# Layer norms on GpSimd: negating the mean in an operation of its own and adding it, instead of subtracting it

## The chip, the cores and the metric

The kernel runs on one core of a Trainium2 chip. The metric is the device time of one execution in microseconds (us); lower is better. The fast runs of one kernel in one group of rounds lie within 0.4% of each other here (4233.40 to 4249.76 us is the widest spread). Ratios are the mean time of one kernel's fast runs over the mean of the other kernel's fast runs of the same rounds, so they are not quite the ratio of the medians that are quoted beside them. A run's state was "fast" everywhere below except where it says otherwise; one run of the kernel before, in the rounds of e5 to e8, was slow (6478.50 us at a clock of 0.827) and counts in no ratio.

The engines are named as in the profile: PE is TensorE (matmuls), PEld its weight loads, DVE VectorE, ACT ScalarE, POOL GpSimd, SP the engine that issues transfers. "L314" is line 314 of the kernel's source. The changed kernel has one more line, so its lines from 311 on are shifted by one.

## The reference

Three transformer layers with a masked attention over a graph, then one graph-attention layer, over a batch of 16 sequences of 1024 nodes with 128 features. What matters here is the norm, which each of the three layers does twice and the last layer once (cut):

```python
def _layer_norm(x, g, b):
    mu = jnp.mean(x, axis=-1, keepdims=True)
    var = jnp.var(x, axis=-1, keepdims=True)
    return (x - mu) * jax.lax.rsqrt(var + LN_EPS) * g + b
# per layer (cut):
scores = jnp.where(mask, -jnp.inf, scores); attn = jax.nn.softmax(scores, axis=-1)
x = _layer_norm(h + (attn_out @ Wo + bo), ln1_g, ln1_b)
x = _layer_norm(x + relu(x @ W1 + b1) @ W2 + b2, ln2_g, ln2_b)
```

All gains are 1 and all shifts 0 in the test's inputs, but the kernel computes them.

## The kernel before

The work is cut into 48 blocks (16 sequences, three layers). A block has 32 steps of attention; each step computes scores for four heads on TensorE, masks and exponentiates them, and multiplies the result with the values on TensorE. Between the steps, the rest of another block (projections, norms, feed-forward, the last layer) is threaded in piece by piece. The norms work on half a sequence at a time: four tiles of 128 rows and 128 features, called a half-norm here. There are 224 of them.

The statistics are VectorE's, the rest of the norm GpSimd's:

```python
def stats(n, ts):
    z, st, mv = n
    for t in range(ts.start, ts.stop):
        nc.vector.bn_stats(st[:, t, :], z[:, t, :])
    for t in range(ts.start, ts.stop):
        nc.vector.bn_aggr(mv[:, t, :], st[:, t, :])       # mean, variance

def normalise(n, ts):                                     # L307 to L314
    z, _, mv = n
    v = mv[:, ts, 1]
    nc.gpsimd.tensor_scalar(v, v, EPS, None, op0=OP.add)
    nc.gpsimd.tensor_tensor(v, v, half_neg[:, ts], OP.pow)
    for t in range(ts.start, ts.stop):
        nc.gpsimd.tensor_scalar(z[:, t, :], z[:, t, :], mv[:, t, 0:1], mv[:, t, 1:2],
                                op0=OP.subtract, op1=OP.mult)
```

GpSimd also masks part of each step's exponentials, and TensorE's next product waits for that:

```python
if on_pool:                                               # in score_step; cut
    nc.scalar.activation(ev, psv, AF.Exp, scale=HD ** -0.5)     # L401
    nc.gpsimd.tensor_mul(ev, ev, m)                             # L402
else:
    nc.vector.tensor_add(ev, psv, m)                            # L404
# later, in av_step:
nc.tensor.matmul(acc[...], v_bufs[m % 2][...], e[:, j, :], start=first, stop=last)   # L421
```

## Time and profile before

| | before |
|---|---|
| time, median of 4 runs | 4239.91 us (4233.33 to 4242.12) |
| span in the profile | 4234.7 us |
| PE busy | 3816.1 us, 90% |
| GpSimd busy | 3698.5 us, 87% |
| of it the norm tiles (L314) | 700.8 us, 896 of 795 ns |
| mean granted TensorE clock | 0.983 of full speed |

"Busy" adds up the durations of an engine's instructions. The share alone doesn't say which engine sets the time; for that one reads the chain of work that ended last, and then single stretches of the timeline. The lines themselves stand in the prediction below.

### The profile page before, as it was taken

To read this page: it belongs to the slowest core of one execution; us is meant where nothing else is said; L and a number is where in the kernel's file an instruction comes from. 1 tells how busy PE (TensorE), PEld (TensorE's weight loads), DVE (VectorE), ACT (ScalarE), POOL (GpSimd) and SP (SyncE) were. 2 spreads that over 40 slices of the span, in tenths; PEclk is the share of its full clock that TensorE was granted. 3 is DMA by queue.
4 is the path that set the end of the run, shared out by engine and by line. 5 is a ranking of instruction groups with operands and counts; after the bars stand their busy time and mean duration, and the time that the engine had idled before them with its cause. 6 is when DMAs were issued, how large, how long until landed. Compare 5 with 4: busy or idle time off the path is not lost.

```text
span 4234.7 us, 107443 instructions
## 1 busy us (share of the span) xinstructions
PE 3816.1 (90%) x44501; PEld 1544.2 (36%) x44501; DVE 3405.5 (80%) x5324; ACT 3412.0 (81%) x3961; POOL 3698.5 (87%) x2786
## 2 busy tenths in 40 slices
PE   7999999999998999999999889989999989989986
PEld 2333333344443333334444333333434433333435
DVE  6888888878887888887787888888878787888873
ACT  6988888977778988887777888988777688888760
POOL 4899999988889999997888899998888899999885
PEclk9999999999999999999999999999999999999997
DMA  5221222222211221221222221221222112221200
GB/s 148 66 61 45 57 61 53 49 52 56 64 48 48 61 61 46 56 61 47 56 52 51 61 58 44 61 61 42 52 65 58 47 46 56 61 53 49 52 17 18
DMA packets 126287, 233.09 MB, mean 55 GB/s; under 512 B 36704, under 2 KB 75616, under 8 KB 125792
## 3 DMA queue, kind: packets, MB, share of 16 engines
q1 hardware_dynamic: 122896, 225.14, 21.2%
q8 instruction: 352, 5.77, 0.6%
q10 hardware_dynamic: 2896, 1.01, 0.1%
q14 instruction: 143, 1.17, 0.1%
HBM read 15.54 MB, written 8.39 MB: 6 GB/s over the span
## 4 chain that ended last, share of the span: by engine, by line
POOL 43%; PE 38%; DVE 10%; ACT 4%; issue 4%; DMA 1%; SPq 1%; ACTq 0%; DVEq 0%; POOLq 0%
POOL e L402 20%; PE t L271 15%; PE acc L421 12%; POOL x L314 12%; PE s L394 9%; DVE e L404 5%; POOL mv L312 4%; POOL x L318 2%; ACT e L401 2%; POOL x L319 2%; PE t L260 2%; ACT e L416 1%; DVE st L296 1%; POOL A L435 1%; POOL mv L311 1%
## 5 line engine op out<-in xcount | busy, mean ns | idle before, releaser
L404 DVE TENSOR_TENSOR e<-s,mask_add 128x1024 f32<-128x1024 f32 x2112 | 2501.9, 1211 | 510.0 <-PE s L394 430.0
L416 ACT ACTIVATE e<-e 128x1024 f32<-128x1024 f32 x2112 | 2200.6, 1060 | 387.2 <-DVE e L404 368.9
L402 POOL TENSOR_TENSOR e<-e,mask 128x1024 f32<-128x1024 f32 x960 | 2046.0, 2148 | 300.0 <-ACT e L401 297.2
L421 PE MATMUL acc<-e,v 128*17 128x512 f32 x12288 | 1633.9, 604 | 195.9 <-POOL e L402 152.5
L394 PE MATMUL s<-Wq,Wk 64*128 64x512 f32 x6144 | 1193.5, 457 | 72.3 <-ACT e L401 27.9
L401 ACT ACTIVATE e<-s 128x1024 f32<-128x1024 f32 x960 | 980.7, 1022 | 202.5 <-PE s L394 199.9
L394 PEld LDWEIGHTS s<-Wq,Wk 64*128 64x128 f32 x6144 | 492.8, 186 | 1042.8 <-issue 486.1
L314 POOL TENSOR_SCALAR x<-x,mv 128x128 f32<-128x128 f32 x896 | 700.8, 795 | 22.9
L421 PEld LDWEIGHTS acc<-e,v 128*17 128x17 f32 x12288 | 208.1, 95 | 731.8 <-issue 384.7
L271 PE MATMUL t<-hd,e 128*32 128x129 f32 x8192 | 244.8, 276 | 7.1 <-DVE x L596 3.2
L312 POOL TENSOR_TENSOR mv<-mv,half_neg 128x4 f32<-128x4 f32 x224 | 231.9, 1035 | 18.5
L318 POOL TENSOR_TENSOR x<-x,ln_g 128x1024 f32<-128x1024 f32 x97 | 229.4, 2365 | 12.7 <-PE t L260 12.6
L271 PEld LDWEIGHTS t<-hd,e 128*32 128x32 f32 x8192 | 226.7, 111 | 26.8 <-issue 5.3
L303 DVE TENSOR_TENSOR x<-t,x 128x512 f32<-128x512 f32 x192 | 131.7, 686 | 91.0 <-PE t L271 90.1
L271 PE MATMUL t<-x1T,W 128*32 128x512 f32 x1536 | 202.4, 599 | 2.3 <-DVE hd L546 1.0
L296 DVE BATCH_NORM_STATS2 st<-x 128x6 f32<-128x128 f32 x896 | 196.7, 279 | 3.0
L271 PEld LDWEIGHTS t<-W,hT 128*32 128x32 f32 x6144 | 172.7, 111 | 63.5 <-issue 26.5
L260 PE MATMUL t<-identf,x 128*128 128x128 f32 x896 | 155.0, 298 | 39.6 <-DVE x L303 12.6
L271 PE MATMUL t<-W,hT 128*32 128x128 f32 x6144 | 187.1, 274 | 2.7 <-DVE x L303 1.9
L260 PEld LDWEIGHTS t<-identf,x 128*128 128x128 f32 x896 | 99.1, 146 | 236.5 <-issue 78.4
L311 POOL TENSOR_SCALAR mv<-mv 128x4 f32<-128x4 f32 x224 | 52.6, 235 | 151.7 <-DVE mv L298 137.8
L581 DVE SCALAR_TENSOR_TENSOR e<-s,mask 128x1024 f32<-128x1024 f32 x128 | 150.5, 1210 | 5.9 <-PE s L578 5.0
(82 smaller groups left out, 2438.1 us busy)
## 6 DMA issues: line engine op xcount, KB each, us to landing
Wk<-hi SPq DMA_DIRECT2D x384, 128.0 KB
Wk<-lo SPq DMA_DIRECT2D x384, 128.0 KB
Wq<-hi SPq DMA_DIRECT2D x384, 128.0 KB
Wq<-lo SPq DMA_DIRECT2D x384, 128.0 KB
x<-in_x_dram SPq DMA_DIRECT2D x16, 512.0 KB
out_dram<-x SPq DMA_DIRECT2D x31, 256.0 KB
ai<-in_adj_dram SPq DMA_DIRECT2D x8, 512.0 KB
g_rows<-parts SPq DMA_DIRECT2D x124, 4.0 KB
```

What stands on the lines that cost most here:

```text
L260: nc.tensor.transpose(ps[:, t * P:(t + 1) * P], src[:, 4 * h + t, :], identf)
L271: nc.tensor.matmul(dst[j:j + SLOT, :], lhsT[:, j:j + SLOT], rhs, start=start, stop=stop)
L296: nc.vector.bn_stats(st[:, t, :], z[:, t, :])
L312: nc.gpsimd.tensor_tensor(v, v, half_neg[:, ts], OP.pow)
L314: nc.gpsimd.tensor_scalar(z[:, t, :], z[:, t, :], mv[:, t, 0:1], mv[:, t, 1:2], op0=OP.subtract, op1=OP.mult)
L318: nc.gpsimd.tensor_mul(z, z, rows(gain, n))
L394: nc.tensor.matmul(ps[:, r * 512:(r + 1) * 512], k[64 * r:64 * r + 64, kt * P:(kt + 1) * P], q[64 * r:64 * r + 64, q0:q0 + 512], start=Tru ...
L401: nc.scalar.activation(ev, psv, AF.Exp, scale=HD ** -0.5)
L402: nc.gpsimd.tensor_mul(ev, ev, m)
L404: nc.vector.tensor_add(ev, psv, m)
L416: nc.scalar.activation(ev, ev, AF.Exp, scale=HD ** -0.5)
L421: nc.tensor.matmul(acc[j * SLOT:j * SLOT + HD + 1, :], v_bufs[m % 2][:, kt, 2 * j + g, :], e[:, j, :], start=first, stop=last)
```

## The change

The idea: if GpSimd's subtraction with a following multiplication runs in a slow form, write the subtraction as the addition of a negated number, and pay for the negation with one small operation per half-norm.

```diff
-        v = mv[:, ts, 1]
+        m, v = mv[:, ts, 0], mv[:, ts, 1]
+        nc.gpsimd.tensor_scalar(m, m, -1.0, None, op0=OP.mult)
         nc.gpsimd.tensor_scalar(v, v, EPS, None, op0=OP.add)
         nc.gpsimd.tensor_tensor(v, v, half_neg[:, ts], OP.pow)
         for t in range(ts.start, ts.stop):
-            nc.gpsimd.tensor_scalar(z[:, t, :], ..., op0=OP.subtract, op1=OP.mult)
+            nc.gpsimd.tensor_scalar(z[:, t, :], ..., op0=OP.add, op1=OP.mult)
```

The order of all other instructions on each engine is the same in both programs.

More of the change, by code (lines that the diff above doesn't have):

```diff
@@ L313, in normalise @@
         for t in range(ts.start, ts.stop):
-            nc.gpsimd.tensor_scalar(z[:, t, :], z[:, t, :], mv[:, t, 0:1], mv[:, t, 1:2], op0=OP.subtract, op1=OP.mult)
+            nc.gpsimd.tensor_scalar(z[:, t, :], z[:, t, :], mv[:, t, 0:1], mv[:, t, 1:2], op0=OP.add, op1=OP.mult)
     def scale_shift(z, gain, bias):
```

## The prediction

> **What bounds the kernel now.** I read the first page from its top. Busy shares and the 40 slices first, to see whether one engine is the bound:
>
> ```profile
> PE 3816.1 (90%) x44501; PEld 1544.2 (36%) x44501; DVE 3405.5 (80%) x5324; ACT 3412.0 (81%) x3961; POOL 3698.5 (87%) x2786
> ...
> PE   7999999999998999999999889989999989989986
> ...
> POOL 4899999988889999997888899998888899999885
> ```
>
> No engine is alone at the top. TensorE (PE) is busy 90% of a span of 4234.7 us and GpSimd (POOL) 87%, and both stay at 8 to 9 tenths in nearly every slice: there is no stage with a limit of its own, the whole run is one steady interleaving. Next the chain that ended last, to see how those two share the path:
>
> ```profile
> POOL 43%; PE 38%; DVE 10%; ACT 4%; issue 4%; DMA 1%; SPq 1%; ACTq 0%; DVEq 0%; POOLq 0%
> POOL e L402 20%; PE t L271 15%; PE acc L421 12%; POOL x L314 12%; PE s L394 9%; DVE e L404 5%; POOL mv L312 4%; POOL x L318 2%; ACT e L401 2%; POOL x L319 2%; PE t L260 2%; ACT e L416 1%; DVE st L296 1%; POOL A L435 1%; POOL mv L311 1%
> ```
>
> The path changes hands: GpSimd 43%, TensorE 38%. Line 314, the one that the change edits, has 12% of it, some 508 us. The groups of GpSimd's instructions by line give its busy time as 700.8 us, so about 508/700.8 = 0.72 of its time lies on the path. For line 312 the same quotient is 0.04 x 4234.7 / 231.9 = 0.73.
>
> The groups by line, kept apart by shape, give the price of each operation that the change touches or that I compare with:
>
> ```profile
> L402 POOL TENSOR_TENSOR e<-e,mask 128x1024 f32<-128x1024 f32 x960 | 2046.0, 2148 | 300.0 <-ACT e L401 297.2 <-DMA Wq<-lo 1.9
> L314 POOL TENSOR_SCALAR x<-x,mv 128x128 f32<-128x128 f32 x896 | 700.8, 795 | 22.9
> L312 POOL TENSOR_TENSOR mv<-mv,half_neg 128x4 f32<-128x4 f32 x224 | 231.9, 1035 | 18.5
> L311 POOL TENSOR_SCALAR mv<-mv 128x4 f32<-128x4 f32 x224 | 52.6, 235 | 151.7 <-DVE mv L298 137.8 <-DVE chk L326 13.9
> L200 POOL TENSOR_TENSOR b<-b,row 128x128 f32<-128x128 f32 x3 | 1.4, 458 | 15.6 <-DMA row<-in_L_gnn_ln_b_dram 15.6
> ```
>
> Line 314 is 896 one-tensor operations of 128 elements at 795 ns. Line 200, an operation with two tensors on the same 128x128 shape, takes 458 ns. So line 314, with one tensor to read and not two, takes 1.7 times as long. That oddity is what the whole prediction hangs on.
>
> Last the timeline of GpSimd over one group of four tiles and the stretches of 10 us around such bursts:
>
> ```profile
> 2004.82 0.25 POOL L311 TENSOR_SCALAR mv<-mv 128x4 f32<-128x4 f32 x1
> 2005.15 1.04 POOL L312 TENSOR_TENSOR mv<-mv,half_neg 128x4 f32<-128x4 f32 x1
> 2006.29 3.13 POOL L314 TENSOR_SCALAR x<-x,mv 128x128 f32<-128x128 f32 x4
> 2009.39 0.23 POOL L311 TENSOR_SCALAR mv<-mv 128x4 f32<-128x4 f32 x1
> ```
>
> ```profile
> 2060.00:2070.00 10.00, 6.31 (x60) 2.77 (x56) 8.44 (x25) 4.92 (x5) 9.63 (x13) 0.83 0.01 2
> 2070.00:2080.00 10.00, 10.00 (x80) 3.15 (x72) 8.66 (x16) 9.20 (x12) 9.65 (x10) 1.00 0.27 79
> 2080.00:2090.00 10.00, 6.53 (x40) 1.69 (x36) 5.57 (x7) 5.91 (x7) 10.00 (x6) 0.83 0.01 2
> ```
>
> From start to start a norm of four tiles takes 9.39 - 4.82 = 4.57 us: 0.33 for adding EPS, 1.14 for the power, 3.10 for four tiles (775 ns each). The stretches (columns: stretch, its length, busy us of PE, PEld, DVE, ACT, POOL, then clock, DMA share, GB/s) show what several such norms in a row do: GpSimd is full, 9.63 to 10.00 us of 10, and PE falls to 6.31 and 6.53 us. Where norms cluster, GpSimd is the bound; where they don't, it waits for ScalarE (297.2 us before line 402) and TensorE is dense.
>
> **What the Trainium skill says.** "GPSIMD Engine Reference", section 3.1 "Elementwise — side-by-side cycle accounting", puts a loop body with one or two ALU operations at 1.03 cycles per element, and an operation with two input tensors at about 2.6 because both inputs share one read port; section 4.1 "Engine selection" calls one-input operations roughly line-rate. The trace agrees on two inputs: line 402 takes 2148 ns for 1024 elements against 458 for 128, a slope of 1690/896 = 1.89 ns, or 2.26 cycles at the 1.2 GHz of that page's section 1; lines 318 and 319, without the broadcast over two halves, take 2388 ns for 1024 and 1284 for 512, 2.16 ns or 2.59 cycles. On one input the trace disagrees strongly: a 4-element operation (line 311) takes 235 ns, so 128 elements at 1.03 cycles should take some 235 + 124 x 0.86 = 342 ns (an estimate from that page); line 314 takes 795. Either about (795 - 235)/124 = 4.5 ns an element are spent, 5.4 cycles, or part of it is a fixed cost of two scalar operands read from memory; section 7 "Performance pitfalls for Q7 kernels" gives some 102 cycles for a read command that doesn't pipeline, so two would be an estimated 170 ns, which leaves 390 ns for 124 elements, still 3.1 ns or 3.8 cycles each. In both readings line 314 runs in some slow form. No page says that a subtraction is slower than an addition.
> "Perfetto Trace Analysis", section "GPSIMD Engine Instruction", advises to time GpSimd from start to start. Here it makes little difference: 775 against 795 ns.
>
> **The change part by part.**
> Added: one operation per four tiles, of the kind of line 311, on the means instead of the variances: 224 of them. At 235 ns that is 53 us; at the 0.33 us from start to start that line 311 needs when its successor waits for it, 74 us. The negation is not needed by the next instruction but only by the third one after, and so may cost nearer to 235; I take 60 us. It stands in front of the power on the same engine, in order, so nothing hides it except GpSimd's own idle time. With the 0.72 from the chain: 0.72 x 60 = +43 us.
> Removed: nothing by count. 896 operations change from subtract and multiply to add and multiply. By the shape alone nothing changes. If the slow form of line 314 is the subtraction's, the addition would run between the 342 ns estimated above and some 590 (235 + 170 for two scalar reads + 128 elements at 1.8 cycles, the rate that section 3.1 gives for a tight loop, 192 ns). The middle, 465 ns, saves 330 ns: 896 x 0.33 = 296 us of GpSimd's busy time; less 60 us it is a net 236 us.
> Moved: no buffer, transfer, wait of another engine or order of work. The mean's column is overwritten in place, and only lines 311 to 314 read it after the statistics are done.
> How much of 236 us reaches the end: not 0.72, because TensorE takes over as GpSimd gets shorter. TensorE's idle time is 4234.7 - 3816.1 = 419 us in all, and 152.5 us of it wait for line 402, more for what follows the norms. I take 0.55: 236 x 0.55 = 130 us, so 4239 - 130 = 4109 us.
>
> **The rivals.**
> A: addition and subtraction cost the same, and the slowness of line 314 belongs to two operations in one, or to its scalar operands. For it: no page mentions such a difference, and lines 318 (multiply) and 319 (add) cost the same to within 0.1%, so this engine need not tell simple operations apart. Against: one-tensor operations should be near line-rate, and here one of two simple ALU operations is all that distinguishes this line from that; also, nobody would add an operation without expecting to gain from it. Then only the added 60 us count: 4239 + 43 = 4282 us, 1.0% slower.
> B: the addition is faster, but TensorE is the bound just behind. For it: PE is at 90%, and in the dense stretches at 10.00 of 10. Then a pass-through of 0.25 instead of 0.55: 236 x 0.25 = 59 us, 4180 us, 1.4% faster, and called the same. Against: PE is only busy 6.3 to 6.5 of 10 us where norms cluster, and these are the places where the time is given back.
> C: the gain is hidden because VectorE and ScalarE (80 and 81%) fill up, since faster norms let the next block's work arrive sooner. They have about 820 us of slack each; I give this little weight, it is a part of the 0.55.
> D: the negation waits on the previous or holds up the next operation, since means and variances interleave in one tile and an overlap may be seen between them: then 224 x 0.66 us for the pair as against 0.33, the 74 us above, 0.72 x 74 = +53 us in case A. That is 1.3%, still within 2%.
>
> **Range and chances.** I hold it 0.6 likely that addition runs in a faster form. Within that: per-operation savings from 205 (at 590 ns) to 453 ns (at 342) give net GpSimd savings of 124 to 346 us; times 0.55 that is 68 to 190 us, so 4171 to 4049 us. About 0.85 of this branch lies beyond 2% (below 4154 us): 0.51. The other branch, 0.4, is 4270 to 4292 us, and the rest of the first branch is within 2% too. Slower by over 2% would need over 85 us from 224 small operations, 380 ns each on the path: 0.03. The two branches leave a hole near 4200; the range must cover both ends: 4045 to 4290. For one number I stay in the likelier branch and lean a little to the other: 4125 us.
>
> **What would show it.** In the changed kernel's groups by line, the row of the 128x128 TENSOR_SCALAR decides: at 350 to 600 ns the first branch is right, at 780 to 800 rival A. The negation must appear as 224 rows of about 235 ns; start to start of its pair tells D. GpSimd's busy total should be near 3698 - 236 = 3460 us (first branch) or 3755 (A). In the chain, GpSimd's 43% should fall below TensorE's share in the first branch. If the row falls and the time does not, B is right. I would be wrong altogether if addition came out slower than subtraction, or if GpSimd's other rows changed.

## The result, and the profile after

The changed kernel takes 4125.16 us (4120.31 to 4128.09, four runs), 114.75 us less than before: ratio 0.9731, 95% interval 0.9714 to 0.9748.

Busy shares of the changed kernel, and its chain that ended last (by engine, then by line):

```profile
PE 3819.7 (93%) x44501; PEld 1548.1 (38%) x44501; DVE 3405.9 (83%) x5324; ACT 3393.8 (82%) x3961; POOL 3445.7 (84%) x3010
...
PE 47%; DVE 19%; ACT 12%; POOL 12%; issue 9%; DMA 1%; SPq 0%; ACTq 0%; DVEq 0%; POOLq 0%
PE t L271 18%; PE acc L422 15%; PE s L395 11%; DVE e L405 11%; POOL e L403 6%; ACT e L402 5%; ACT e L417 5%; DVE st L296 2%; PE t L260 2%; POOL x L315 2%; DVE lo L360 2%; DVE x L303 1%; ACT xT L265 1%; DVE tt L433 1%; POOL x L319 1%
```

GpSimd's busy time fell by 252.8 us. The work of the other engines is what it was, to within 0.6%; PE's 3816 and 3820 us are equal, it only waits less. In the chain GpSimd fell from 43% to 12%; TensorE, VectorE and ScalarE have the path now. The norm's tiles fell from 12% of the path to 2%.

GpSimd's groups of instructions by line (count, busy us, mean ns of one, idle time before them and what ended it):

```profile
L315 POOL TENSOR_SCALAR x<-x,mv 128x128 f32<-128x128 f32 x896 | 389.2, 448 | 24.0
L313 POOL TENSOR_TENSOR mv<-mv,half_neg 128x4 f32<-128x4 f32 x224 | 231.9, 1035 | 18.5
...
L311 POOL TENSOR_SCALAR mv<-mv 128x4 f32<-128x4 f32 x224 | 52.8, 236 | 167.5 <-DVE mv L298 137.4 <-DVE chk L327 15.8
L312 POOL TENSOR_SCALAR mv<-mv 128x4 f32<-128x4 f32 x224 | 50.7, 226 | 15.1
```

A norm tile takes 448 ns, not 795: 700.8 - 389.2 = 311.6 us saved. The small operations (L311 negates now, L312 adds EPS) take 52.8 + 50.7 us where one row of 52.6 stood, 50.9 us more. And in time, one half-norm from GpSimd's timeline (start, duration, engine, line, operation):

```profile
2017.29 0.24 POOL L311 TENSOR_SCALAR mv<-mv 128x4 f32<-128x4 f32 x1
2017.59 0.23 POOL L312 TENSOR_SCALAR mv<-mv 128x4 f32<-128x4 f32 x1
2017.90 1.04 POOL L313 TENSOR_TENSOR mv<-mv,half_neg 128x4 f32<-128x4 f32 x1
2019.05 1.73 POOL L315 TENSOR_SCALAR x<-x,mv 128x128 f32<-128x128 f32 x4
```

From its start to that of the next operation the negation takes 0.30 us; the four tiles last 1.73 us against 3.13. The whole half-norm, from its first start to the end of its last tile, went from 4.60 us to 3.49 us.

Stretches of 10 us of the changed kernel around such norms (columns as in the prediction):

```profile
2010.00:2020.00 10.00, 8.01 (x174) 4.78 (x166) 6.82 (x26) 3.03 (x3) 9.30 (x16) 1.00 0.01 2
2020.00:2030.00 10.00, 9.28 (x86) 3.79 (x86) 8.33 (x16) 7.39 (x9) 9.27 (x15) 0.83 0.10 29
2030.00:2040.00 10.00, 9.26 (x76) 2.79 (x72) 8.57 (x10) 10.00 (x13) 9.89 (x9) 1.00 0.18 52
```

GpSimd is still full here, but PE is busy 8.0 to 9.3 us of 10; in the kernel before it had been at 6.3 and 6.5, with one full stretch between. By the count of VectorE's masked additions this is the same work: from the 1062nd to the 1076th of them 30.3 us passed before (2061.1 to 2091.5) and 25.8 after (2016.8 to 2042.6).

**Where the time went.** GpSimd runs its instructions one after the other, in the order of the program, in every timeline here. A mask multiplication that is queued behind a half-norm starts when the last norm tile has ended, and TensorE's next product waits for the mask. The timelines of the kernel before and of the changed one at the same place of the same block show it; the square brackets hold the idle time of the engine and what ended it. Before:

```profile
457.37 3.13 POOL L314 TENSOR_SCALAR x<-x,mv 128x128 f32<-128x128 f32 x4
...
459.87 0.73 PE L394 MATMUL s<-Wq,Wk 64*128 64x512 f32 x4
...
460.46 2.13 POOL L402 TENSOR_TENSOR e<-e,mask 128x1024 f32<-128x1024 f32 x1
...
462.65 1.05 PE L421 MATMUL acc<-e,v 128*17 128x512 f32 x8 [2.04 <-POOL e L402]
```

After:

```profile
451.17 1.74 POOL L315 TENSOR_SCALAR x<-x,mv 128x128 f32<-128x128 f32 x4
...
452.88 2.17 POOL L403 TENSOR_TENSOR e<-e,mask 128x1024 f32<-128x1024 f32 x1
...
454.09 0.73 PE L395 MATMUL s<-Wq,Wk 64*128 64x512 f32 x4
...
455.10 1.05 PE L422 MATMUL acc<-e,v 128*17 128x512 f32 x8 [0.27 <-POOL e L403]
```

TensorE's wait for the mask went from 2.04 to 0.27 us. Over the whole run, the list of waits (us in total, times, longest) has this of it before, after, and in run e2 below:

```profile
PE acc L421 <- POOL e L402: 152.5, 141, 4.4
PE acc L422 <- POOL e L403: 25.9, 39, 2.4
PE acc L421 <- POOL e L402: 208.2, 126, 5.3
```

The change took away 126.6 us of such waits, against 108.4 us of span.

To see where in the run, I took from the trace the starts of VectorE's 2112 masked additions, 44 for each block. (A block lasts from the last of the block before to its own last.) Of the 48 blocks, 25 are ordinary (only projections, norms and feed-forward threaded in), 20 carry last-layer work too, and the first three (64 to 79 us) stand apart. Most ordinary blocks take 78.4 us before and 76.1 us after, the 25 together 1962.5 and 1905.7 us: 57 us. The 20 others together take 1892.8 us before and 1846.1 after, 47 us. The rest of the 108 us, 5 us, lies almost all behind the last block. So the gain is spread over the run, as PE's slices in the first page suggested.

### The profile page after: what moved, and what is told of

Read it like the earlier page. It is cut to its first block, busy times and chain, and to the rows that moved or that the text cites. A ratio compares the mean times of both kernels' runs of the same rounds, so it can differ in the third digit from the quotient of the medians.

```text
span 4126.3 us, 107667 instructions
## 1 busy us (share of the span) xinstructions
PE 3819.7 (93%) x44501; PEld 1548.1 (38%) x44501; DVE 3405.9 (83%) x5324; ACT 3393.8 (82%) x3961; POOL 3445.7 (84%) x3010
## 4 chain that ended last, share of the span: by engine, by line
PE 47%; DVE 19%; ACT 12%; POOL 12%; issue 9%; DMA 1%; SPq 0%; ACTq 0%; DVEq 0%; POOLq 0%
PE t L271 18%; PE acc L422 15%; PE s L395 11%; DVE e L405 11%; POOL e L403 6%; ACT e L402 5%; ACT e L417 5%; DVE st L296 2%; PE t L260 2%; POOL x L315 2%; DVE lo L360 2%; DVE x L303 1%; ACT xT L265 1%; DVE tt L433 1%; POOL x L319 1%
## 5 line engine op out<-in xcount | busy, mean ns | idle before, releaser
L403 POOL TENSOR_TENSOR e<-e,mask 128x1024 f32<-128x1024 f32 x960 | 2049.3, 2150 | 395.4 <-ACT e L402 392.7
L395 PE MATMUL s<-Wq,Wk 64*128 64x512 f32 x6144 | 1209.0, 459 | 80.3 <-ACT e L402 34.9
L315 POOL TENSOR_SCALAR x<-x,mv 128x128 f32<-128x128 f32 x896 | 389.2, 448 | 24.0
L260 PE MATMUL t<-identf,x 128*128 128x128 f32 x896 | 150.9, 292 | 55.4 <-DVE lo L360 27.4
L311 POOL TENSOR_SCALAR mv<-mv 128x4 f32<-128x4 f32 x224 | 52.8, 236 | 167.5 <-DVE mv L298 137.4
L260 PEld LDWEIGHTS t<-identf,x 128*128 128x128 f32 x896 | 97.0, 144 | 251.9 <-issue 96.5
```

The source lines that it names most:

```text
L260: nc.tensor.transpose(ps[:, t * P:(t + 1) * P], src[:, 4 * h + t, :], identf)
L395: nc.tensor.matmul(ps[:, r * 512:(r + 1) * 512], k[64 * r:64 * r + 64, kt * P:(kt + 1) * P], q[64 * r:64 * r + 64, q0:q0 + 512], start=Tru ...
```

## The experiments

Twelve kernels ran. Six questions: which form is slow (1), what each half of the change is worth (2, 3, 4), whether TensorE is the bound behind GpSimd (8), whether the place of the small operation matters (5, 9), whether the negation is better on another engine (6, 7, 12), and whether its form matters (10, with 11 as its base). The "before" of each round ran on the same chip. The table leaves out e1, which has no time of use.

| run | edit | median us | ratio to before | GpSimd busy us |
|---|---|---|---|---|
| e2 | negation's cost alone, subtraction kept | 4343.70 | 1.0262 | 3756.0 |
| e9 | the same at the tail | 4344.25 | 1.0245 | 3759.5 |
| e5 | an operation meant for the tail, moved to the start | 4284.23 | 1.0102 | 3754.9 |
| before | | 4234.61 to 4242.35 | 1 | 3698.5 |
| e7 | changed, negation and EPS on VectorE | 4237.76 | 0.9991 | 3345.6 |
| e4 | half the tiles added | 4196.07 | 0.9909 | 3603.6 |
| e6 | changed, negation on VectorE | 4145.37 | 0.9773 | 3397.3 |
| changed (e11) | | 4125.64 | 0.9729 | 3445.7 (first profile) |
| e10 | changed, small operations in pair form | 4115.45 | 0.9703 | 3425.8 |
| e12 | changed, negation as a reduction on VectorE | 4109.19 | 0.9685 | 3395.8 |
| e3 | addition alone (wrong result) | 4098.51 | 0.9675 | 3391.2 |
| e8 | changed, no gain | 4101.78 | 0.9674 | 3188.6 |

### e1: which form is slow

The kernel before with blocks of eight single operations behind its end, for instance:

```diff
+    for i in (0, 1, 2, 3) * 2:   # L779; one such block for each form, fz 128x512, fm 128x4x2
+        nc.gpsimd.tensor_scalar(fz[:, i*128:(i+1)*128], fz[:, i*128:(i+1)*128],
+                                fm[:, i, 0:1], fm[:, i, 1:2], op0=OP.subtract, op1=OP.mult)
```

> The kernel before, with blocks of 8 single GpSimd operations appended behind its end, each form on a line of its own, to read the cost of each form by itself. Theory 1 (the subtraction is what runs slowly on GpSimd's one-tensor operation): 128x128 subtract-mult 795 ns and add-mult 448 ns as in the two kernels; mult-add, add-add, mult-mult near 448; mult-subtract near 795; a subtraction alone 300 ns or more above an addition alone; 128x512 subtract-mult near 2500 ns, add-mult near 1100. Theory 2 (one pair, add then mult, has a form of its own, and everything else is slow): mult-add, add-add, mult-mult and max-mult near 795 too, and subtraction alone equal to addition alone. Theory 3 (the scalar operands read from memory cost the time): the forms with immediate scalars lie 150 ns or more below those with scalars from memory, for subtraction and addition alike. Two-tensor subtract against add: equal under theories 2 and 3, open under 1.

The result was correct. (One look, state unknown, 4320.31 us with the added operations; its time is of no use.) GpSimd's groups by line, the same columns as above:

```profile
L801 POOL TENSOR_SCALAR fz<-fz,fm 128x512 f32<-128x512 f32 x8 | 16.6, 2072 | 0.8
...
L779 POOL TENSOR_SCALAR fz<-fz,fm 128x128 f32<-128x128 f32 x8 | 6.2, 797 | 0.1
...
L803 POOL TENSOR_SCALAR fz<-fz,fm 128x512 f32<-128x512 f32 x8 | 6.1, 767 | 0.5
L797 POOL TENSOR_SCALAR fz<-fz 128x128 f32<-128x128 f32 x8 | 4.9, 649 | 0.0
L789 POOL TENSOR_SCALAR fz<-fz,fm 128x128 f32<-128x128 f32 x8 | 4.7, 626 | 0.0
...
L787 POOL TENSOR_SCALAR fz<-fz,fm 128x128 f32<-128x128 f32 x8 | 4.7, 618 | 0.0
...
L781 POOL TENSOR_SCALAR fz<-fz,fm 128x128 f32<-128x128 f32 x8 | 3.5, 453 | 0.0
...
L799 POOL TENSOR_SCALAR fz<-fz 128x128 f32<-128x128 f32 x8 | 2.1, 303 | 0.0
```

The lines stand for these forms; the table adds the ones not shown, from the same view:

| form at 128x128 | ns, scalars from memory | ns, scalars in the instruction |
|---|---|---|
| subtract, mult | 797 (L779) | 649 (L797) |
| mult, subtract | 805 | |
| add, add | 800 | |
| max, mult | 810 | |
| add, mult | 453 (L781) | 303 (L799) |
| mult, add | 457 | |
| mult, mult | 463 | |
| subtract alone | 618 (L787) | 529 |
| add alone | 626 (L789) | 534 |
| mult alone | 629 | |
| two tensors, subtract / add | 453 / 453 | |

At 512 columns subtract-mult takes 2072 ns (L801) and add-mult 767 (L803). So the slopes are (2072 - 797)/384 = 3.32 ns an element against (767 - 453)/384 = 0.82, and what is left at no elements is about 372 against 348 ns: the fixed cost is nearly the same, the rate differs by a factor of four.

What follows: neither theory 1 nor theory 2 holds as it stood. Subtraction by itself is no slower than addition by itself, and add-add is as slow as subtract-mult; that fells theory 1. But not add-mult alone is fast: mult-add and mult-mult are too. The tested pairs fall in two classes, three fast (add-mult, mult-add, mult-mult) and four slow, and every single operation tested is slow, slower than a fast pair that does more. Theory 3 holds as an extra: scalars from memory cost 148 to 150 ns more than scalars in the instruction, for slow and fast pairs alike. Why there are two classes no run shows.

### e2, e3, e4: the two halves of the change

```diff
 e2: the small operation alone, with a factor that changes nothing
+        m = mv[:, ts, 0]; nc.gpsimd.tensor_scalar(m, m, 1.0, None, op0=OP.mult)
 e3: the addition alone, no negation: wrong result on purpose
-  op0=OP.subtract, op1=OP.mult)
+  op0=OP.add, op1=OP.mult)
 e4: two tiles of four added (their means negated), two subtracted: right result
+        m = mv[:, ts.start:ts.stop:2, 0]; nc.gpsimd.tensor_scalar(m, m, -1.0, None, op0=OP.mult)
+  op0=(OP.subtract if t % 2 else OP.add), op1=OP.mult)
```

> The kernel before with the added operation alone: the mean is multiplied by +1.0 and still subtracted (right result). It measures what the negation costs. From the prediction's working: 224 operations, GpSimd's busy time up by 51 us (3750), 0.72 of 60 us on the path: about 4282 us, ratio 1.010. Rival: the small operations fall into GpSimd's idle time and cost under 10 us, ratio under 1.003.

> The kernel before with the addition alone and no negation; the result is wrong on purpose (x + mean). GpSimd's busy time near 3395 us. If what is taken from GpSimd goes on reaching the end at 0.45 (115 us of 253 so far), the further 51 to 69 us are worth 23 to 31 us: 4095 to 4102 us, ratio 0.966 to 0.968. If they are worth 0.72: 4075 us, 0.961. If TensorE already bounds the changed kernel: 4115 to 4125 us, ratio 0.971 to 0.973.

> Two of each four tiles are added (their means negated), the other two still subtracted; right result. GpSimd's busy time about 3698 - 448 x 0.347 + 51 = 3594 us, 104 us less. If the time follows GpSimd's busy time on a straight line through the two kernels (0.45): 4240 - 47 = 4193 us, ratio 0.989. If the first microseconds taken are worth more than the last (0.72, then TensorE takes over): 4240 - 75 = 4165 us, ratio 0.982.

e2 took 4343.70 us (4339.60 to 4348.66), ratio 1.0262 with an interval of 1.0245 to 1.0279: 109 us more than the 4234.61 us of before, for 57.5 us more of GpSimd's busy time. Both expectations missed it. e3 took 4098.51 us, ratio 0.9675 (0.9659 to 0.9691), as expected from a pass-through (the share of GpSimd's saved time that reaches the end) of 0.45. e4 took 4196.07 us, ratio 0.9909 (0.9893 to 0.9926): about 38 us saved by the ratio, somewhat less than the 47 us (0.989) of the straight line, and far from the 0.982 of the other reading.

So the small operation costs 109 us in front of subtractions and about 24 us in front of additions (the ratios 0.9731 and 0.9675 of the changed kernel and e3, times 4235 us). The two halves don't add up: -136 us for the addition alone, +109 for the small operation alone, but -115 together. On the side of less work the line is nearly straight (by the ratios, 0.41 us for each microsecond of GpSimd from before to e4, 0.48 from e4 to the changed kernel). On the side of more work it is four times as steep: 109/57.5 = 1.9 us for each microsecond.

The timeline of e2, at the place shown above of the two kernels, shows what is new:

```profile
465.39 3.14 POOL L314 TENSOR_SCALAR x<-x,mv 128x128 f32<-128x128 f32 x4
...
468.50 2.13 POOL L402 TENSOR_TENSOR e<-e,mask 128x1024 f32<-128x1024 f32 x1
...
470.68 1.05 PE L421 MATMUL acc<-e,v 128*17 128x512 f32 x8 [2.47 <-POOL e L402]
...
471.67 0.93 PE L260 MATMUL t<-identf,x 128*128 128x128 f32 x4
...
472.52 1.22 PE L394 MATMUL s<-Wq,Wk 64*128 64x512 f32 x4
```

The stall is 2.47 us, 0.43 more than before. And after it the matmuls run slower: the transposes of L260 take 0.93 us, the scores of L394 1.22, where they took 0.66 and 0.73 in the kernel before after its stall. Short stretches of e2 (length, then PE, PEld, DVE, ACT, POOL busy us, then the granted clock) say why:

```profile
470.00:472.00 2.00, 1.32 (x11) 0.47 (x12) 0.34 (x1) 0.98 (x2) 2.00 (x3) 0.98 0.77 199
472.00:474.00 2.00, 2.00 (x11) 0.84 (x13) 0.14 (x1) 1.34 (x2) 2.00 (x2) 0.50 0.79 205
```

The granted clock fell to one half. The Trainium skill, "TensorE: Matmul & The Clock Gate", section "Part 1: The HAM clock gate (the "warmup" mystery)", describes this: TensorE runs at half its clock after at least one idle window of about 3.4 us, and a free-running window decides. The trace agrees on the halving; but here a stall of 2.47 us was enough, so a stall of 3.4 us is not needed in this kernel. Counting in the traces between 200 and 4000 us: before has 46 PE stalls over 1.5 us, 15 of them followed by the half clock within 3.5 us of their end; e2 has 85, 44 of them followed by it (during the stall counts too). Time at half clock, whole run: 150.0 us before, 283.9 us in e2, 124.9 us in the changed kernel. The two parts can be told apart. PE's busy time itself grew by 45 us, and its waits for the mask by 56 us (152.5 to 208.2): together 101 of the 103 us by which e2's span is longer.

The ordinary blocks show the same, since some of them in e2 ran at the full clock throughout. Before, none of the 25 has any half clock, and they take 78.5 us on average. In e2 the 5 without half clock take 80.1 us, the 16 with 3.4 us of it 81.2, and the 4 with 6.8 us of it 82.3. An ordinary block has four half-norms, so four of the small operations, 1.2 us in all. At full clock they lengthen it by 1.6 us, as much as its waits for the mask grew (from 3.6 to 5.2 us); each 3.4 us of half clock adds another 1.1. Over the 25 blocks that makes about 24 x 1.1 = 26 of 66 us. So the clock makes the slope steeper, but the longer waits are the larger part. This is a comparison of blocks within one run; no run of its own held the clock fixed.

### e5 and e9: does the place of the small operation matter

```diff
 e5: after the four tiles, on a tile that nothing else reads
+        nc.gpsimd.tensor_scalar(pad[:, :, 0], pad[:, :, 0], 1.0, None, op0=OP.mult)
 e9: after the four tiles, on the means that they have read
+        nc.gpsimd.tensor_scalar(mv[:, ts, 0], mv[:, ts, 0], 1.0, None, op0=OP.mult)
```

> The kernel before with 224 small GpSimd operations of the same kind and shape as the negation, but at the tail of each group of four norm tiles and on a tile that nothing else reads. It asks whether the 109 us of the run with the factor +1.0 come from the load on GpSimd or from the place at the head of the norm. Theory of load (GpSimd sits at a limit in the kernel before, more work there opens TensorE stalls that also lower its granted clock): about +100 us, ratio 1.022 to 1.028, granted clock near 0.97. Theory of place (the head of the norm delays what follows from it): about the prediction's +43 us or less, ratio 1.005 to 1.010, granted clock near 0.98.

e5 took 4284.23 us, ratio 1.0102 (1.0078 to 1.0126), which looks like the theory of place. It isn't: the trace shows that all 224 operations ran between 16.2 and 89.1 us after the start. Nothing tied them to the norms, so the scheduler had put them first, and they delayed the first mask once (the longest single wait of VectorE is 44.0 us). The run tells nothing about place.

> The repair of the run with the extra operation at the tail, whose operations the scheduler had moved to the start of the program: here the extra operation multiplies the mean by +1.0 after the four norm tiles that read it, so it must stay there, and nothing reads it afterwards (right result). If the cost is that the mask multiplication queued on GpSimd behind the norm starts later, the tail costs what the head costs: about +100 us, ratio 1.022 to 1.028, granted clock near 0.97. If the cost is that the norm's own result comes later, the tail is nearly free: ratio under 1.008, granted clock near 0.98.

e9 took 4344.25 us, ratio 1.0245 (1.0226 to 1.0263), clock 0.969 in the profile: the same as e2 at the head. So it is not the norm's own tiles that come too late, but what is queued behind them on GpSimd. PE's waits for the mask, 216.6 us here, say that this is the masks above all; other work of GpSimd that stands in the same queue was not separated.

### e8: is TensorE the bound behind GpSimd

```diff
-        nc.gpsimd.tensor_mul(z, z, rows(gain, n))      # in the changed kernel
```

> The changed kernel without the multiplication by the gain, which is 1 in these inputs (so the result is right here, not in general). It takes 270 us more off GpSimd (near 3175 us busy) and touches nothing else. If 0.45 of it still reaches the end: 122 us, about 4000 us, ratio 0.944. If TensorE bounds the changed kernel (rival B of the prediction): under 40 us, ratio 0.964 to 0.972.

4101.78 us, ratio 0.9674 (0.9649 to 0.9699). GpSimd's busy time fell by another 257 us, as much as the change itself had brought, and the time fell by only about 23 us against the changed kernel (ratios 0.9674 and 0.9729 in e11). The ordinary blocks take 76.1 us in the changed kernel, in e3 and in e8 alike: there neither 54 nor 257 us less of GpSimd's work changes anything. Nearly all that e3 and e8 gain over the changed kernel lies in the 20 blocks with last-layer work: 1846.1 us in the changed kernel, 1821.9 in e3, 1822.7 in e8. Very different amounts of GpSimd's work (54 us and 257 us) bring the same gain; so from here on it counts where the work is, not how much it is in sum. PE is busy 93% in both.

### e6, e7 and e12: the negation on VectorE

```diff
 e6, in stats(), no negation on GpSimd:
+        nc.vector.tensor_scalar(mv[:, ts, 0], mv[:, ts, 0], -1.0, None, op0=OP.mult)
 e7, besides, and no EPS on GpSimd:
+        nc.vector.tensor_scalar(mv[:, ts, 1], mv[:, ts, 1], EPS, None, op0=OP.add)
 e12, instead of e6's operation:
+        nc.vector.tensor_reduce(mv[:, ts, 0], mv[:, ts, 0:1], AX.X, OP.add, negate=True)
```

> The changed kernel with the negation moved to VectorE, behind the statistics (right result). GpSimd's busy time near 3391 us as in the run without the negation. If VectorE's 224 small operations hide in its 17% of idle time: ratio 0.967 to 0.969, as there. If VectorE's order of work delays the path: 0.972 or more, nothing gained over the changed kernel.

> As the one before, with the addition of EPS moved to VectorE as well (right result). GpSimd's busy time near 3340 us. At 0.45 of what GpSimd is relieved of (53 to 74 us more): 24 to 33 us more, ratio 0.960 to 0.962. If TensorE bounds from here on: 0.966 to 0.968, no better than the one before.

e6 took 4145.37 us, ratio 0.9773 (0.9753 to 0.9792), slower than the changed kernel; e7 4237.76 us, ratio 0.9991 (0.9984 to 0.9998), the whole gain gone. GpSimd's busy time did fall to 3397.3 and 3345.6 us. The cause is in the duration of VectorE's small operation. The view of e6's line (operation, count, shortest, median and longest in ns, first and last start):

```profile
L299 DVE TENSOR_SCALAR mv<-mv x256: 115/164/2119, 124.9 to 4132.5; 128x4 f32<-128x4 f32 x89, 128x2 f32<-128x2 f32 x39
```

The median is 164 ns, but the longest is 2119, about the length of one mask multiplication on GpSimd (2150 ns); the mean of the 128x4 ones is 431 ns, in e7 516. The long ones wait for GpSimd: 86 of e6's 256 took over 0.4 us (82.6 us in all), and each of them began while a GpSimd operation ran (77 times a mask multiplication) and ended 22 to 32 ns after the end of that one. Not every operation of GpSimd holds them: 97 began during its power, L312, and none of these took over 166 ns. The Trainium skill, "SBUF — State Buffer", section "Who interferes with whom", says that GpSimd and VectorE share a pair of memory ports as an exclusive lock, that a tensor_scalar on VectorE may take the pair, and that a reduction never contends on trn2. e12 tests just that:

> The negation on VectorE again, but as a reduction over one element with its sign turned, an operation that the Trainium skill lists as never contending for the port pair shared with GpSimd. If the 0.4 us mean (up to 2.1 us) of the former version's negation came from waiting for a GpSimd instruction to end, this one takes 100 to 200 ns each with a maximum under 0.4 us, VectorE's busy time stays under 3450 us, and the time comes to the run without the negation: ratio 0.967 to 0.970, better than the changed kernel's 0.973. If VectorE's order is what costs, 0.975 to 0.978 again.

```profile
L299 DVE TENSOR_REDUCE mv<-mv x256: 97/145/159, 123.0 to 4096.5; 128x4 f32<-128x4 f32 x89, 128x2 f32<-128x2 f32 x39
```

The longest is 159 ns now, VectorE's busy time 3419.9 us against e6's 3487.6, and the time 4109.19 us (4099.12 to 4115.20), ratio 0.9685 (0.9666 to 0.9704), with a right result. 111 of the reductions began during a mask multiplication, and 101 of them ended before it did. The same work at the same place in another form: it is the form of the operation, and not VectorE's order, that made e6 slow. That the lock of the skill is behind it fits the ends of the long operations, but the lock itself is not seen in a trace. TensorE's waits for VectorE's masked additions went with it: 22.9 us in the changed kernel, 39.4 in e6, 105.6 in e7, 14.6 in e12. e12 beats the changed kernel in the same rounds (4125.64, 4122.38 to 4129.34; no run of one overlaps with the other) by 16 us or 0.4%, and comes within 0.1% of e3 (0.9675), which does no negation at all. It is the fastest version found that is right for any gain.

### e10 and e11: the form of the small operations

```diff
+        nc.gpsimd.tensor_scalar(m, m, -1.0, 0.0, op0=OP.mult, op1=OP.add)
+        nc.gpsimd.tensor_scalar(v, v, 1.0, EPS, op0=OP.mult, op1=OP.add)
```

> The changed kernel with its two small operations written as a multiply-add pair with immediate scalars (mean times -1 plus 0; variance times 1 plus EPS), the form whose 128 elements took 303 ns against 530 for a single operation; right result. If the fast form helps at 4 elements too, each takes about 200 ns in place of 226 to 236, 2 x 224 x 0.03 = 13 us of GpSimd, and at most 6 us of time: ratio 0.971 to 0.973. If the per-element rate is all that differs, 4 elements save nothing: equal to the changed kernel.

> The changed kernel again, with the two statements on one line so that the line numbers stay, for a comparison in the same rounds: ratio 0.973, between 0.971 and 0.975.

e11 repeated the result: 4125.64 us, 0.9729 (0.9714 to 0.9744). e10 took 4115.45 us (4113.16 to 4118.07), 0.9703 (0.9688 to 0.9718): 10 us less than e11; no run of one overlaps with the other, though the intervals of the two ratios overlap slightly. A pair with a useless second operation is faster than the single operation even at four elements: 198 and 196 ns against 236 and 226. From start to start that is 0.26 and 0.28 us in place of 0.30 and 0.31, about 0.07 us a half-norm or 16 us in all, of which more reached the end than the 6 us that I had expected.

## Why the prediction was right, and where it wasn't

**The time: right, and partly by luck.** 4125.0 was predicted, 4125.16 measured. The number was the likelier branch's 4109 us moved by hand toward the other branch; the branch itself was 16 us too low.

**What bounds the kernel: right.** The path did change hands between GpSimd and TensorE, and the gain was made where norms cluster. The stall of 2.04 us that became 0.27 shows the mechanism: masks queued behind norms.

**The form of the norm tiles: the conclusion right, its reason wrong.** "Line 314 runs in some slow form" holds. That the slow form is the subtraction's does not: subtraction alone is as fast as addition alone (618 and 626 ns), and add-add is as slow as subtract-mult. It is the pair that decides. The saving of 330 ns by estimate was 347 ns. The fast rate of 0.82 ns, 0.98 cycles at 1.2 GHz, is in effect the 1.03 of "GPSIMD Engine Reference", section 3.1. The estimate of 342 ns for the whole operation was too low because it took the 235 ns of line 311, a single operation without scalars from memory, as the fixed cost, which is 348 ns for the fast pair. The two scalars from memory, estimated at 170 ns, cost 150. Two of the prediction's readings are looser than they sound: its 2.26 cycles an element come from two different instructions (lines 402 and 200), so they say little about the page's 2.6, and lines 318 and 319 agree to 0.4% (2380 to 2388 ns), not to 0.1%.

**The negation: right in length.** 60 us were assumed, 50.9 us more busy time and 0.30 us x 224 = 67 us from start to start were measured. In the changed kernel it is worth about 24 us of time (e3), not 0.72 x 60.

**How much reaches the end: the size was off.** 0.55 was assumed. Measured: 114.75/252.8 = 0.45. A net of 236 us of GpSimd was predicted, 252.8 measured. The two errors partly cancel.

**Rival A: the step that failed.** Its size was "0.72 x 60 = +43 us", hence 4282 us, and hence 0.03 for slower. e2 is that case, and took 4344 us, 2.6% slower. Had the addition been no faster, the change would have lost by over 2%, and the chance for that should have been near the 0.4 that rival A had. The mistake was to take a line's share of the chain as the price of one more microsecond on that line. The share says what the path was made of. More work there lengthened TensorE's waits for the mask by 56 us, and far more stalls were followed by the half clock (44 against 15), which lengthened its matmuls by 45 us: 101 us where 43 had been put.

**Rival B: right in part.** Ordinary blocks end at a floor of 76.1 us in three kernels with GpSimd busy from 3189 to 3446 us. The change reaches that floor and no more; a further 257 us taken from GpSimd brought 23 us (e8). What the floor is made of was not taken apart: PE is at 93% there, VectorE and ScalarE at 82 to 83% and on the chain.

**Rival C: visible.** VectorE and ScalarE rose from 10 and 4% to 19 and 12% of the chain. How much of the lost pass-through is theirs is not separated. **Rival D: near in length** (the two small operations take 0.61 us from start to start, 0.66 was given), wrong in time for the same reason as rival A.

## What to carry to other kernels

When an instruction costs much more per element than its neighbours on the same engine, measure its forms one by one before explaining it: here a pair with one useless operation beats a single one, and a small change of algebra moves an instruction from one class to the other. Price added and removed work separately, and at the operating point: the same 0.3 us operation cost 109 us where TensorE was already stalling behind GpSimd, and about 24 us where most of those stalls were gone. When small work is moved to VectorE beside a busy GpSimd, look at its longest duration, not only at its median.

## What the Trainium skill lacked or had wrong

- "GPSIMD Engine Reference", section 3.1: no word that one-tensor operations with scalars fall in two classes. Measured at 128x128 with scalars from memory: add-mult, mult-add, mult-mult 453 to 463 ns; subtract-mult, mult-subtract, add-add, max-mult 797 to 810; the slopes of one pair of each class are 0.82 and 3.32 ns an element. The 1.03 cycles of that page fit the fast class alone.
- The same page, section 4.1, calls one-input operations roughly line-rate: a single addition of 128 elements took 626 ns with its scalar from memory and 534 with it in the instruction, two tensors added 453 (fixed costs included).
- The same page, section 7: a scalar operand's price is not listed. Two of them from memory cost 148 to 150 ns more than two in the instruction.
- "TensorE: Matmul & The Clock Gate", section "Part 1: The HAM clock gate (the "warmup" mystery)", names an idle window of about 3.4 us: here stalls of 1.5 to 2.7 us were followed by the half clock in part of the cases (35 of 75 in e2 between 1.5 and 2.7 us).
- "SBUF — State Buffer", section "Who interferes with whom", was right on the masks: a small tensor_scalar took up to 2119 ns beside GpSimd, a reduction of the same elements at most 159 ns. Beside GpSimd's 128x4 power, though, no tensor_scalar was held up (97 cases, at most 166 ns). The page does not say that the reduction with its sign turned can stand in for a negation.
